# A 7x7 depthwise convolution as one matrix product per tile of pixels, with v laid out in ten dense planes

## The chip, the cores and the metric

The kernel runs on one core of one Trainium2 chip. The metric is the time of one execution on the device in microseconds, lower being better; for a comparison several executions are made and their median is taken. A core has a matrix engine (TensorE, in the profile PE, with its weight loads as PEld), a vector engine (VectorE, DVE), an engine for activations and copies (ScalarE, ACT), a general engine (GpSimd, POOL) and an engine that here issues most of the DMA transfers (SyncE, SP). Each engine executes its own instructions in order and waits on semaphores for what the others produce. SBUF is the memory on the core, PSUM the memory into which matrix products go, HBM the large memory[...].

## The reference

The input `x` has 4 images of 256 channels and 64 x 64 pixels, in float32. Two layers follow each other, each with a group normalization in front and a residual sum behind. The first layer (A below) is an attention of 8 heads of 32 channels over keys and values that come from two 2x2 convolutions of stride 2. The second layer (B) is an attention within each quarter of an image (an area of 16 rows), plus a depthwise 7x7 convolution of its values, and a projection. The part that the change touches is in the second layer:

```python
def _L1_conv_ref(x, w_qkv, b_qkv, w_pe, b_pe, w_proj, b_proj):
    ...
    def _dwconv7(x, w, b):
        y = lax.conv_general_dilated(x, w, window_strides=(1, 1), padding=[(3, 3), (3, 3)], dimension_numbers=('NCHW', 'OIHW', 'NCHW'), feature_group_count=x.shape[1])
        return y + b[None, :, None, None]
    ...
    out = jnp.einsum('bhij,bjhd->bihd', attn, v)
    out = out.reshape(B, N, C)
    v_full = v.reshape(B, N, C)
    out = out.reshape(B, H, W, C).transpose(0, 3, 1, 2)
    v_full = v_full.reshape(B, H, W, C).transpose(0, 3, 1, 2)
    out = out + _dwconv7(v_full, w_pe, b_pe)
    return _conv1x1(out, w_proj, b_proj)
...
x = x + _L0_conv_ref(_gn(x), L0_conv_Wq, L0_conv_Wk, L0_conv_Wv, L0_conv_rel_h, L0_conv_rel_w)
x = x + _L1_conv_ref(_gn(x), L1_conv_w_qkv, L1_conv_b_qkv, L1_conv_w_pe, L1_conv_b_pe, L1_conv_w_proj, L1_conv_b_proj)
```

Each channel has its own 49 taps, and the edges are padded with zeros by 3 pixels.

## The kernel before

**The main loop.** The work is cut into 8 blocks (layer A for the images 0 to 3, then layer B for the images 0 to 3) of 16 units each, 128 units in all. A unit is one chunk of 512 queries (8 rows of an image) and four heads; it has 8 steps, one for each 128 keys. One step issues, in this order: the four score products `s` (`scores`, L261, four row groups side by side), the first of two exponentials on ScalarE (L265), the four products `av` of the step before (`weighted`, L272, four column groups side by side), the second exponential, what the plan holds for this step, and then one or more parts of the side queue. VectorE sums the exponentials of a unit (L797), and after the last step the products with `ones` (`den`, L281) give the divisors. The PSUM tiles of `s` and `den` come from three buffers, all side work shares one PSUM buffer (`side`, L163).

**The plan.** The order is written out by hand. `at(g, j, f)` puts a function into step j of unit g; `task(parts, f)` puts side work of so many parts on the queue `side`, and a function yields where a part ends. In the main loop (L804 to L837) a step takes one part when anything waits, a second when more than 7 parts wait and a third when more than 14 do, one fewer in step 2; further parts in the same step must be of the same task. `need` (L191) takes parts off the queue until something is made. Side parts are the projections of layer A (`k0ps`, `v0ps`, `q0ps`) and B (`k1ps`, `q1ps`), the values of layer B (`vals_ps`), the convolution (`conv_ps`) and the last projection (`ops`). `product` (L151) makes each as four matmuls of 32 output channels side by side.

**The values of layer B.** `plan_values` (L644) loads a chunk of `xmid` (`hv`), normalizes it on ScalarE (L243), makes the products, evicts them with the bias into `vout` (L669, rows of 72 floats: 64 pixels with zeros around them), and, after the second half of the channels, stores the chunk twice: four transfers into `vala` (L677), from which `load_v` and `make_v` (L497, L503) take the values for the attention, and eight, one per row, into `vals` (L682), which holds all rows of all channels and images with the halo, from the last row to the first. The start of each image's chunks in units is given at L771: image 0 from 17.8, image 1 from 48.3, image 2 from 49.8, image 3 from 65.8, with 3.4, 1.0, 1.6 and 0.4 units from chunk to chunk. Before the first of them `plan_zeros` (L616) writes the halo rows of `vals`, zeroes `bands` and puts the taps in with seven transfers.

**The convolution.** `plan_conv` (L695) runs for 64 groups of four channels, from unit 70.5 on, 0.52 units apart. It loads 42 rows of `vals` for each half of the image, three times with a shift of 0, 1 and 2 pixels, into 126 partitions of `rows` (six transfers, L705), and for every second group a tile `band` with the taps as a band matrix (three transfers, L717). For each of two channel pairs and three groups of column shifts it makes four matmuls of 126 rows, 32 output rows and 256 columns (L732: four images of 64 pixels), accumulated over the three column shifts; the task has three parts. One copy (L739) brings 512 columns to SBUF, two transfers (L741) to `conv`. The first load waits with `need(stored, ...)` until the last chunk of values is planned out.

**The rest.** For the images 0 to 2 the attention's result is put aside in `attd` (L548). From unit 105.28 on, 0.8 units apart, `load_rest` (L554) loads a chunk of `conv` (one transfer, L556) and of `attd`, `add_conv` four steps later adds them with the bias (L572), and `project` makes the projection and adds the residual (L583) before `out` is stored (L586). Image 3 does the same behind its own attention.

**DMA.** All these transfers are issued by SyncE in program order. Each takes one of eight semaphores in turn and waits for the transfer that used it last.

## Time and profile before

| | us |
|---|---|
| median of 3 runs | 3268.01 (3267.55 to 3268.94) |
| the profiled execution | 3270.47 |
| its span, from the first to the last instruction | 3268.7 |
| TensorE busy | 3218.2 |
| ScalarE busy | 2525.6 |
| VectorE busy | 2491.6 |
| GpSimd busy | 487.2 |
| exponentials (L265), 2048 of 1027 ns | 2016.9 |
| sums of exponentials (L797), 1792 of 1219 ns | 2113.3 |
| convolution matmuls (L732), 3072 | 195.1 |
| their evictions (L739), 64 of 587 ns | 37.5 |

The granted clock of TensorE was 0.997 over the span. The busy time of a group is the union of its instructions, so concurrent matmuls are counted once; a mean is that of one instruction, and four matmuls that run side by side have each their full length. An f32 matmul of the program stands as two instructions in the trace. In lines of groups the columns are the line, engine and operation, the tiles out<-in with their shapes, the number of instructions, then the busy time and the mean in ns, then the idle time before and what ended it. In timelines they are the start in us, the length, the engine and line, and the tiles.

The DMA page lists 319,853 packets and 397.27 MB, at a mean of 122 GB/s. SyncE's transfers take 38.5% of the sixteen DMA engines' time. A transfer is cut into packets, one for each contiguous run of bytes.

The units of the convolution stage last from about 1787 us (unit 71) to 2663 us (unit 105).

### The profile page before, as it was taken

To read this page: it belongs to the slowest core of one execution; us is meant where nothing else is said; L and a number is where in the kernel's file an instruction comes from. 1 tells how busy PE (TensorE), PEld (TensorE's weight loads), DVE (VectorE), ACT (ScalarE), POOL (GpSimd) and SP (SyncE) were. 2 spreads that over 40 slices of the span, in tenths; PEclk is the share of its full clock that TensorE was granted. 3 is DMA by queue.
4 is the path that set the end of the run, shared out by engine and by line. 5 is a ranking of instruction groups with operands and counts; after the bars stand their busy time and mean duration, and the time that the engine had idled before them with its cause. 6 is when DMAs were issued, how large, how long until landed. Compare 5 with 4: busy or idle time off the path is not lost.

```text
span 3268.7 us, 72561 instructions
## 1 busy us (share of the span) xinstructions
PE 3218.2 (98%) x29730; PEld 961.1 (29%) x29730; DVE 2491.6 (76%) x2621; ACT 2525.6 (77%) x2993; POOL 487.2 (15%) x923
## 2 busy tenths in 40 slices
PE   7999999999999999999999999999999999999997
PEld 4233323333233322222222333333333322222221
DVE  3777897779877787778876767666776778888887
ACT  3888788887888888888887777777777787776765
POOL 0111121111211111111111111111111111111111
PEclk9999999999999999999999999999999999999999
DMA  5312212313322213553236667676766643445431
GB/s 179 80 64 73 77 66 90 100 59 116 100 69 84 65 63 91 148 138 113 82 120 158 162 151 178 159 174 141 180 171 153 172 142 123 166 147 172 155 121 57
DMA packets 319853, 397.27 MB, mean 122 GB/s; under 512 B 182652, under 2 KB 215708, under 8 KB 319192
## 3 DMA queue, kind: packets, MB, share of 16 engines
q1 hardware_dynamic: 291064, 356.06, 38.5%
q0 software_dynamic: 28448, 36.48, 4.2%
q8 instruction: 236, 3.87, 0.5%
q14 instruction: 105, 0.86, 0.1%
HBM read 285.98 MB, written 106.42 MB: 120 GB/s over the span
## 4 chain that ended last, share of the span: by engine, by line
PE 94%; DMA 2%; issue 1%; ACT 1%; DVE 1%; SPq 0%; POOL 0%; DVEq 0%; ACTq 0%; POOLq 0%
PE s L261 33%; PE av L272 29%; PE conv_ps L732 5%; PE den L281 4%; PE k0ps L155 3%; PE k1ps L155 3%; PE q1ps L155 3%; PE v0ps L155 3%; PE q0ps L155 3%; PE ops L155 3%; PE vals_ps L155 3%; ACT p L265 1%; DVE p L797 1%; DMA conv<-cout 0%; DMA rows<-vals 0%
## 5 line engine op out<-in xcount | busy, mean ns | idle before, releaser
L797 DVE TENSOR_TENSOR p<-p 128x1024 f32<-128x1024 f32 x1792 | 2113.3, 1219 | 623.1 <-ACT p L265 583.3
L265 ACT ACTIVATE p<-s 128x1024 f32<-128x1024 f32 x2048 | 2016.9, 1027 | 571.9 <-PE s L261 564.0
L261 PE MATMUL s<-q,k_A 32*128 32x512 f32 x4096 | 608.2, 640 | 1.4 <-ACT p L265 0.9
L261 PE MATMUL s<-q,k_B 32*128 32x512 f32 x4096 | 588.7, 640 | 1.1 <-ACT p L265 0.8
L272 PE MATMUL av<-p,v_A 128*32 128x512 f32 x4096 | 551.1, 603 | 0.0
L272 PE MATMUL av<-p,v_B 128*32 128x512 f32 x4096 | 546.0, 604 | 0.0
L308 POOL DMA_DIRECT2D rb<-recs x508 | 252.4, 502 | 454.1 <-DMA recs<-few 377.5
L306 POOL DMA_DIRECT2D recs<-few x127 | 70.2, 553 | 1423.2 <-DVE sums L305 1372.1
L261 PEld LDWEIGHTS s<-q,k_A 32*128 32x128 f32 x4096 | 176.3, 183 | 357.8 <-issue 273.3
L261 PEld LDWEIGHTS s<-q,k_B 32*128 32x128 f32 x4096 | 162.5, 182 | 363.3 <-issue 290.5
L272 PEld LDWEIGHTS av<-p,v_A 128*32 128x32 f32 x4096 | 89.4, 108 | 383.0 <-issue 335.0
L272 PEld LDWEIGHTS av<-p,v_B 128*32 128x32 f32 x4096 | 87.6, 108 | 378.8 <-issue 332.9
L732 PE MATMUL conv_ps<-rows,band 126*32 126x256 f32 x3072 | 195.1, 379 | 0.0
L732 PEld LDWEIGHTS conv_ps<-rows,band 126*32 126x32 f32 x3072 | 123.0, 139 | 113.0 <-issue 78.3
L297 POOL DMA_DIRECT2D rows<-den_sb x127 | 74.6, 587 | 433.3 <-ACT den_sb L290 424.1
L281 PE MATMUL den<-p,ones 128*32 128x512 f32 x1024 | 137.8, 605 | 0.4 <-DVE p L797 0.4
L155 PE MATMUL ops<-cv,wp_sb 128*32 128x512 f32 x1024 | 129.8, 600 | 6.0 <-issue 6.0
L155 PE MATMUL vals_ps<-hv,wqkv_sb 128*32 128x512 f32 x1024 | 130.1, 596 | 3.9 <-ACT vout L669 3.8
L155 PE MATMUL k0ps<-taps,wk_sb 128*32 128x256 f32 x2048 | 130.6, 383 | 3.0 <-ACT taps L243 3.0
L155 PE MATMUL k1ps<-h,wqkv_sb 128*32 128x512 f32 x1024 | 128.7, 593 | 2.4 <-ACT cout L739 1.6
L155 PE MATMUL q0ps<-hq,wq_sb 128*32 128x512 f32 x1024 | 129.8, 592 | 0.0
L155 PE MATMUL q1ps<-h,wqkv_sb 128*32 128x512 f32 x1024 | 129.7, 596 | 0.1
(87 smaller groups left out, 1594.9 us busy)
## 6 DMA issues: line engine op xcount, KB each, us to landing
rb<-recs POOLq DMA_DIRECT2D x508, 64.0 KB, 2.4
rows<-vals SPq DMA_DIRECT2D x128, 189.0 KB
rows<-vals SPq DMA_DIRECT2D x128, 188.8 KB
rows<-vals SPq DMA_DIRECT2D x128, 188.7 KB
vala<-vout SPq DMA_DIRECT2D x128, 144.0 KB
vals<-vout SPq DMA_DIRECT2D x256, 72.0 KB
vc<-vala SPq DMA_DIRECT2D x32, 576.0 KB
hq<-in_x SPq DMA_DIRECT2D x32, 512.0 KB
```

What stands on the lines that cost most here:

```text
L155: T.matmul(out[cols, :], lhsT=lhsT[:, cols], rhs=rhs, start=start, stop=stop)
L261: T.matmul(pairs[h // 2][:, h % 2, :], lhsT=k[rows, unit[0], j * P : (j + 1) * P], rhs=q[rows, :], start=True, stop=True,)
L265: exps = [lambda i=i: S.activation(p[i], pairs[i], AF.Exp, scale=SCALE) for i in range(2)]
L272: T.matmul(av[HD * h : HD * h + HD, :], lhsT=v[:, j, unit[0] * P + HD * h : unit[0] * P + HD * h + HD], rhs=p[h // 2][:, h % 2, :], start= ...
L281: T.matmul(dens[g][HD * h : HD * h + HD, :], lhsT=ones, rhs=p[h // 2][:, h % 2, :], start=True, stop=True,)
L297: G.dma_start(rows, den_sb[0:P:HD, :])
L306: G.dma_start(recs.rearrange("h (q n) -> (h q) n", n=CH // HD), few[:, 1, :])
L308: G.dma_start(rb[HD * h : HD * h + HD, :], recs[h : h + 1, :].to_broadcast([HD, CH]))
L732: T.matmul(ps[HD * m : HD * m + HD, i], lhsT=band_tiles[k][:, g, :, part + c], rhs=xs[:, m % 2, c, :, 3 * g : 3 * g + WW], start=(g == 0), ...
L797: soon(1, lambda i=i: V.tensor_add(ps[0][i], ps[0][i], ps[j][i]))
```

## The change

The convolution takes tiles of six by four pixels. The rows of `rows` are now the 12 rows and 10 columns around such a tile (120 partitions), the outputs are 24 pixels (padded to 32) for each channel, and the columns of the product run over the tiles: 11 tile rows, 4 images and 16 tiles across. One matmul per channel gives all its outputs of a half (6 or 5 tile rows, 384 or 320 columns), with no accumulation. For this `vals` in HBM holds ten planes, one for each column offset within the window, each dense; a chunk of values is stored into it with ten transfers per half of the channels (`vals` L698 of the changed kernel), given out after each half and not at the end of the chunk. A half's rows are loaded in one transfer (L732), three halves ahead. `bands` has one band of 19 x 13 taps positions for every 16 channels, filled with 49 transfers and loaded with ten. The pixels of `vout`, `vala`, `conv` and `cv` are ordered by their column modulo four, so the copies that make `k`, the transposes that make `v` and the two sums that use `cv` read or write by columns; the eviction of `k` is split in two, and `conv` is loaded with 16 transfers per chunk. The starts of the values and of the convolution are set anew.

```diff
-BAND = HH // 2 + 2 * HALO
-BROWS = 42
-TC = 8
+TY, TX, NY, XT, NP, TC = 6, 4, 11, WW // 4 + 2, 120, 16
+BY, BX = 12 + 7, 10 + 3
...
-    vals = dram.tile([HH + 2 * HALO + BROWS - BAND, C, B, XP], FP, name="vals")
-    vala = [[dram.tile([4, HD, NH, 4, XP], FP, name=f"vala_{b}_{a}") for a in range(NAREA)] for b in range(B)]
-    conv = dram.tile([C, B, N], FP, name="conv")
-    bands = dram.tile([C // TC, 9, BROWS + HH // 2 - 1, TC], FP, name="bands")
+    vals = dram.tile([TY * NY + 2 * HALO, TX + 2 * HALO, C, B, WW // TX], FP, name="vals")
+    vala = [[dram.tile([4, HD, NH, 4 * TX, XT], FP, name=f"vala_{b}_{a}") for a in range(NAREA)] for b in range(B)]
+    conv = dram.tile([C, HD, NY, B, WW // TX], FP, name="conv")
+    bands = dram.tile([C // TC, BY, BX, TC], FP, name="bands")
...
-            S.activation(
-                k[:, qd, :].rearrange("p (j t i) -> p t j i", t=4, i=32)[:, 2 * half : 2 * half + 2],
-                ps.rearrange("p (t j i) -> p t j i", t=2, i=32), AF.Identity, bias=bqkv_sb[:, 1, qd : qd + 1],
-            )
+            for n in range(2):
+                S.activation(
+                    k[:, qd, :].rearrange("p (r g t f x) -> p t r g f x", r=4, g=2, t=4, f=2)[:, 2 * half + n],
+                    ps[:, n * 256 : (n + 1) * 256].rearrange("p (r x g f) -> p r g f x", r=4, g=2, f=2),
+                    AF.Identity, bias=bqkv_sb[:, 1, qd : qd + 1],
+                )
...
-            nc.sync.dma_start(cv, conv[:, b, c * CH : (c + 1) * CH].rearrange("(t p) n -> p t n", p=P))
+            for y in range(c * RC, (c + 1) * RC):
+                n, r = y // TY, TY - 1 - y % TY
+                for t in range(CT):
+                    nc.sync.dma_start(
+                        cv[:, t, :].rearrange("p (f r x) -> p r f x", f=TX, r=RC)[:, y - c * RC],
+                        conv[t * P : (t + 1) * P, r * TX : (r + 1) * TX, n, b, :],
+                    )
...
-                V.scalar_tensor_tensor(cv[:, t, :], cv[:, t, :], bpe_sb[:, t : t + 1], att[:, t, :], ALU.add, ALU.add)
+                V.scalar_tensor_tensor(
+                    by_column(cv[:, t, :]), by_column(cv[:, t, :]), bpe_sb[:, t : t + 1],
+                    att[:, t, :].rearrange("p (q f) -> p q f", f=TX), ALU.add, ALU.add,
+                )
...
-            for n in range(7):
+            for n in range(NTAP):
                 nc.sync.dma_start(
-                    bands[:, :7, BAND - 1 - n, :].rearrange("k x c -> x k c"),
-                    tap[7 * n : 7 * n + 7, :].rearrange("x (k c) -> x k c", c=TC),
+                    bands[:, TY - 1 + n // 7, TX + HALO + 2 - n % 7, :].unsqueeze(0),
+                    tap[n : n + 1, :].rearrange("o (k c) -> o k c", c=TC),
                 )
...
-                vout = made["v"] = pool.tile([P, CT, RC, XP], FP, tag="rows", name=f"vout_{b}_{c}", bufs=2)
+                vout = made["v"] = pool.tile([P, CT, RC, TX, XT], FP, tag="rows", name=f"vout_{b}_{c}", bufs=3)
...
+            for n in range(2):
+                nc.sync.dma_start(
+                    vala[b][c // 2][2 * (c % 2) + n, :, 4 * t : 4 * t + 4].rearrange("c h f x -> h c (f x)"),
+                    vout[:, t, 4 * n : 4 * n + 4].rearrange("p r f x -> p (r f x)"),
+                )
+            for dc in range(TX + 2 * HALO):
+                x, f = divmod(dc + TX - HALO, TX)
+                nc.sync.dma_start(
+                    vals[HALO + c * RC : HALO + (c + 1) * RC, dc, t * P : (t + 1) * P, b, :].rearrange("r p x -> p r x"),
+                    vout[:, t, :, f, x : x + WW // TX],
+                )
             if t == CT - 1:
                 stored[b, c] = True
-                for n in range(2):
-                    for tt in range(CT):
-                        nc.sync.dma_start(
-                            vala[b][c // 2][2 * (c % 2) + n, :, 4 * tt : 4 * tt + 4].rearrange("c h r x -> h c (r x)"),
-                            vout[:, tt, 4 * n : 4 * n + 4, :].rearrange("p r x -> p (r x)"),
-                        )
-                for r in range(RC):
-                    nc.sync.dma_start(
-                        vals[HALO + HH - 1 - c * RC - r, :, b, :].rearrange("(t p) x -> p t x", p=P), vout[:, :, r, :]
-                    )
...
+    halves = ((0, 6), (6, NY))
+    def load_band(k):
+        band = band_tiles[k] = pool.tile([NP, 8, TX * TC], FP, tag="band", name=f"band_{k}", bufs=2)
+        for dc in range(10):
+            nc.sync.dma_start(
+                band[dc::10],
+                bass.AP(
+                    tensor=bands.tensor, offset=bands.offset + (k * BY * BX + 9 - dc) * TC,
+                    ap=[[BX * TC, 12], [BX * TC, 8], [1, TX * TC]],
+                ),
+            )
+    def load_rows(n, half):
+        need(stored, (B - 1, NCH - 1))
+        (lo, hi), row, size = halves[half], C * B * WW // TX, 4 * B * WW // TX
+        loaded[n, half] = xs = pool.tile([NP, 6, 4, B, WW // TX], FP, tag="rows", name=f"rows_{n}_{half}", bufs=3)
+        nc.sync.dma_start(
+            xs.rearrange("p y c b x -> p y (c b x)")[:, : hi - lo],
+            bass.AP(
+                tensor=vals.tensor, offset=vals.offset + TY * lo * 10 * row + n * size,
+                ap=[[row, NP], [TY * 10 * row, hi - lo], [1, size]],
+            ),
+        )
+        if half == 0 and n % (TC // 4) == 1 and n < C // 4 - TC // 4:
+            load_band(n // (TC // 4) + 1)
+    def convolve(n, half):
+        if (n, half) not in loaded:
+            load_rows(n, half)
+        xs, (k, part), (lo, hi) = loaded.pop((n, half)), divmod(4 * n, TC), halves[half]
+        size = (hi - lo) * B * WW // TX
+        ps = ps_side(f"conv_ps_{n}_{half}")[:, :size]
+        for m in range(4):
+            T.matmul(
+                ps[HD * m : HD * m + HD].rearrange("p (y b x) -> p y b x", b=B, x=WW // TX),
+                lhsT=band_tiles[k].rearrange("p y (x c) -> p (y x) c", c=TC)[:, :, part + m],
+                rhs=xs[:, : hi - lo, m], start=True, stop=True,
+            )
+        out = pool.tile([P, 6 * B * WW // TX], FP, tag="cout", name=f"cout_{n}_{half}", bufs=2)[:, :size]
+        S.copy(out, ps)
+        nc.sync.dma_start(
+            conv[4 * n : 4 * n + 4].rearrange("c m y b x -> (c m) y (b x)")[:, lo:hi],
+            out.rearrange("p (y x) -> p y x", y=hi - lo),
+        )
+        n, half = divmod(2 * n + half + 3, 2)
+        if n < C // 4:
+            load_rows(n, half)
+        yield
...
-        at(0, when, load)
-        at(0, when + 4, lambda: task(3, convolve))
-    begin, pace = 70.5, 0.52
+        for half in range(2):
+            if n + half < 2:
+                at(0, int(start * NKT) + 2 * half, lambda half=half: load_rows(n, half))
+            if n + half == 0:
+                at(0, int(start * NKT) - NKT, lambda: load_band(0))
+            at(0, int(start * NKT) + 4 + 2 * half, lambda half=half: task(1, convolve, n, half))
+    begin, pace = 71.3, 0.5
...
-            plan_values(b, c, ends[b] + 1.8 + (14.5 if b == 1 else 0) + (3.4, 1.0, 1.6, 0.4)[b] * c)
+            plan_values(b, c, (17.8, 41, 54.5, 65.8)[b] + (3.0, 1.6, 1.25, 0.5)[b] * c)
```

## What was predicted before the changed kernel ran

> **What bounds the kernel now.** I read the page's first two parts, then the chain of waits, the groups by form, the timeline of TensorE inside the convolution, the stretches by stage, and last the SyncE queue around the stores of v. Parts 1 and 4 first:
>
> ```profile
> PE 3218.2 (98%) x29730; PEld 961.1 (29%) x29730; DVE 2491.6 (76%) x2621; ACT 2525.6 (77%) x2993; POOL 487.2 (15%) x923
> ...
> PE 94%; DMA 2%; issue 1%; ACT 1%; DVE 1%; SPq 0%; POOL 0%; DVEq 0%; ACTq 0%; POOLq 0%
> ```
>
> TensorE is on the chain for 94% of the span. Nothing else is over 77% busy, so time taken out of TensorE is worth its length as long as ScalarE and VectorE keep up and no transfer is late. The stretches by stage (columns: us, PE, PEld, DVE, ACT, POOL, granted clock, DMA share, GB/s) say where:
>
> ```profile
> 1603.00:1787.00 184.00, 182.03 (x1456) 46.47 (x1452) 133.76 (x154) 149.59 (x178) 28.40 (x53) 0.99 0.43 121
> 1787.00:2663.00 876.00, 874.44 (x8772) 294.23 (x8768) 612.94 (x595) 663.50 (x762) 125.79 (x239) 1.00 0.68 163
> 2663.00:3043.00 380.00, 379.92 (x3148) 95.66 (x3144) 318.91 (x343) 278.88 (x310) 54.96 (x105) 1.00 0.45 151
> ```
>
> The middle line is the convolution stage: TensorE full, ScalarE at 76%, DMA at 68%. Its timeline shows the rhythm:
>
> ```profile
> 2209.76 1.14 PE L261 MATMUL s<-q,k_B 32*128 32x512 f32 x8
> 2210.83 1.06 PE L272 MATMUL av<-p,v_B 128*32 128x512 f32 x8
> 2211.72 1.05 PE L732 MATMUL conv_ps<-rows,band 126*32 126x256 f32 x16
> 2212.70 1.14 PE L261 MATMUL s<-q,k_B 32*128 32x512 f32 x8
> ```
>
> A step is one `s`, one `av` and what the side queue adds. With 16 convolution matmuls it lasts 2.94 us (2209.76 to 2212.70). Over all 1023 step starts in the trace, a step with no side part is 2.066 us at least (mean 2.314, ScalarE paces it), with one 512-column part 2.925, with 16 convolution matmuls 2.940, with 32 of them 3.806. So a side part costs only its streaming: four matmuls side by side take 0.429 us per pass of 512 columns (0.859 over two passes), that is 0.839 ns a column, and 0.217 us per pass of 256 columns. An f32 product is two passes.
>
> The last views are the queue of SyncE while image 3's v is stored (its timeline), the chain over one chunk, and the tiles' issue times (ns, least, median, most):
>
> ```profile
> 1690.83 1.68 SPq L677 DMA_DIRECT2D vala<-vout  x3
> 1692.55 5.79 SPq L682 DMA_DIRECT2D vals<-vout  x8
> ```
>
> ```profile
> 1691.99 5.97 DMA vala<-vout
> ...
> 1697.98 2.70 DMA vals<-vout
> ```
>
> ```profile
> L682 SPq DMA_DIRECT2D vals<-vout x256: 359/615/2145, 542.6 to 1786.0; - x128
> L677 SPq DMA_DIRECT2D vala<-vout x128: 503/522/1252, 535.1 to 1778.6; - x128
> L741 SPq DMA_DIRECT2D conv<-cout x128: 574/586/1739, 1809.1 to 2654.9; - x128
> ```
>
> One chunk's stores occupy the queue and the transfers for 8.7 us. The last is issued at 1786.0, the first row load follows it, and the first convolution matmul runs at 1797.9: that hand-over has almost no slack.
>
> [...] matmuls on different column groups of 32 run at once. The trace agrees (four such matmuls start about 7 ns apart), so the convolution is priced by columns, not by matmuls. [...] its packets of 1152 B (53 ns each) go at 80 per us there. [...] The trace has 4-byte packets at 5.9 ns per engine (`tap`, 595 in 0.5 us on 7 engines) and 256-byte packets at 15.7 ns (`conv`, 255 in 0.25 us on 16); no run shows 64 B. [...] The trace's only strided f32 read, `taps` with every second element, took 638 ns for 256 elements where the contiguous groups (819 for 512, 1242 for 1024) give 0.61 us by their slope: no penalty at that stride.
>
> **The change part by part.** Sums are against the profiled execution: 3270.5 us, span 3268.7 and 1.8 around it. The median of the runs shown is 3268.0, 2.5 lower, and I subtract that at the end.
>
> 1. *The matmuls.* Before: 12 passes of 256 columns for each of 64 groups of four channels, in 108 steps of 16 matmuls and 42 of 32. They cost 108 x (2.940 - 2.066) + 42 x (3.806 - 2.066) = 94.4 + 73.1 = 167.5 us. After: two halves of 384 and 320 columns, two passes each, one part per step in 128 steps: 64 x 2 x (384 + 320) x 0.839 ns = 75.6 us. Saved: 91.9 us. The instruction order of the changed program, priced step by step this way, gives 92.1 less. Weight loads stay hidden if 32 columns take the 139 ns shown, since a pass now lasts 0.27 to 0.32 us.
>
> 2. *ScalarE.* Eviction copies: 64 of 587 ns become 64 of 384 and 64 of 320 columns; from 371 ns at 256 columns and 589 at 512 these are 0.479 and 0.425, together +20 us. `k` in two halves: 64 x 689 ns become 128 x about 0.47, +16 us. In the convolution stage that makes about (663.5 + 28) of 784 us, 88%: TensorE still ends last there. The single `side` PSUM buffer now changes hands every step, so each copy must end within the 2 us of the next `s` and `av`; behind two exponentials of 1.03 us it just does. I take +4 us; bounds 0 and 35 (1 us for each of 34 units, as units of little side work show). Four more steps without a side part: +1.
>
> 3. *Values moved in time.* Image 2 began at unit 49.8 and ScalarE waited for its normalization:
>
> ```profile
> L243 ACT ACTIVATE hv<-hv,norm_B 128x512 f32<-128x512 f32 x64 | 52.3, 819 | 7.5 <-POOL norm_B L234 7.5
> ```
>
>    That wait made unit 50 take 6.9 us too long. From 54.5 it is gone; image 3's at 65.8 stays. But units 48 to 64 lose side work, and seven more of them drop to 20.8 us of TensorE, where units have taken 0.9 more because ScalarE paces them: +6.3. Net 0.
>
> 4. *The stores of v.* Per half chunk: 2 `vala` as before and 10 transfers of 1024 packets of 64 B in place of 4 of 256 packets of 288 B; 655,360 small packets instead of 65,536. For images 0, 1 and 2 a chunk has 1.25 units (28 us) or more, which hides them. Image 3 has half a unit. I price a 64-byte packet at 7.1 ns per engine[...], an estimate. On the four engines that also carry `vala` a half then takes 64 x 53 ns + 640 x 7.1 ns = 3.4 + 4.5 = 7.9 us; SyncE needs about as much (10 x 0.6 + 2 x 0.52). The same arithmetic for before gives 8.9 us per chunk, against 8.7 seen. In the changed order (steps priced as in 1, counted from the start of unit 64) the halves are ready from 76 to 177 us and the first convolution stands at 194. From 76: 16 x 7.9 = 126, about 16 for the loads of `hv`, `h`, `vc`, `band` among them, 6 for the first row load: 224. TensorE stands 30 us. ScalarE may show part of it earlier, waiting for `hv`, which queues behind the stores; it is the same time. Bounds: 0 (5.9 ns, with the other loads going beside the stores: 76 + 115 is before 194), and 119 with the 15.7 ns of a 256-byte packet.
>
> 5. *Row loads and bands.* 84,480 packets of 1 KB at about 50 ns replace 16,128 of some 0.3 us: 4.2 against 4.8 ms of engine time, hidden as before, three halves (17 us) ahead.
>
> 6. *The start.* 50 instead of 8 `bands` stores, +15 us of SyncE at 0.36 each, ahead of the loads `xa` and `hq` that unit 4 needs; these have some 15 us of lead: +2, bounds 0 and 8.
>
> 7. *The end stage.* `cv` becomes 16 transfers of 0.43 us to issue: 6.9 us, 9.5 to land, against 12.7 us until VectorE adds it. VectorE has 16% free. +3, bounds 0 and 30 (`ops` and `cv` read by columns at twice 745 ns would bring VectorE level with TensorE). The transpose of `v` and the memsets change form alone.
>
> Sum: 3270.5 - 91.9 + 5 + 0 + 30 + 2 + 3 = 3218.6; less 2.5: **3216 us**.
>
> **Rivals.** *No stall*: 64-byte packets stream at 5.9 ns and the other loads fit beside them on the twelve engines without `vala`. For it: 4-byte packets already go at 5.9 ns; against: 8 transfers in flight at most, and `vala` on four engines. Then 3216 - 30 = 3186. *Stores decide* (the slower side): place, the start of the convolution; price per 64-byte packet x, stall = 16 x (3.4 + 0.64 x) - 96. It eats the whole gain of 82 us (92 - 10) from x = 12 ns. For it: the 256-byte packet's 15.7 ns[...]; against: 32-byte stores took 8 ns in the trace, though never many at once. At 15.7 ns: 3268 - 82 + 119 = 3305. *Strided evictions*: ScalarE and VectorE reading PSUM and SBUF by columns pay double; ScalarE in the convolution stage rises by about 1 us per unit and both stages pace on it: 3216 + 31 + 20 = 3267, no change. That the change does not do what it says is out: the order has 4 x 128 matmuls of 384 and 320 columns in place of 1536 of 256.
>
> **How the numbers follow.** Chances: partial stall 0.52 (3195 to 3250), no stall 0.24, stores decide 0.19, strided evictions 0.05. 0.2% (6.5 us) is about what a measurement of this kernel tells from no change. Faster: 0.52 + 0.24 + 0.01 = 0.77; same: 0.04; slower: 0.19. The range must take in the stall-free case below (3182) and most of the way towards the break-even above (3270); beyond it lie perhaps 0.17 of the slower case and a few hundredths below.
>
> **What would show it.** Steps with a convolution of 2.71 and 2.60 us; ScalarE near 88% in that stage; one wait of TensorE for `rows` at the first convolution, of about 30 us, and `vals` on SyncE at 0.6 us each. If `vals` transfers take over 1 us apiece, or ScalarE waits for `hv` through units 67 to 71, the stores decide and I am too low. If steps of the stage stay near 2.9 us, the exposed copies are the cause.

## The result and the profile after

The changed kernel takes 3413.89 us (median of 4 runs, 3400.47 to 3421.40), the kernel before 3267.78 beside it: a ratio of 1.0442, 95% interval 1.0408 to 1.0477. It is 4.4% slower where 3216 us was forecast. The profiled execution took 3410.18 us with a span of 3408.5.

Parts 1 and 4 of the page after, the engine's busy time and the chain of waits:

```profile
PE 3184.7 (93%) x27682; PEld 887.5 (26%) x27682; DVE 2512.6 (74%) x2621; ACT 2542.3 (75%) x3121; POOL 492.0 (14%) x923
...
PE 71%; SPq 11%; DMA 8%; issue 4%; ACT 3%; DVE 3%; POOL 0%; DVEq 0%; ACTq 0%; POOLq 0%
```

TensorE is busy for less time, as intended, but it is on the chain for 71% of the span and no longer 94%. SyncE's queue and transfers, 2% together before, hold it for 19%. ScalarE's share on the chain is 3%.

Where the rows of the convolution were there in time, its matmuls came out as priced. This is TensorE's timeline in the convolution (start, length, both us):

```profile
2239.73 0.88 PE L749 MATMUL conv_ps<-rows,band 120*32 120x384 f32 x8
2240.55 1.24 PE L263 MATMUL s<-q,k_B 32*128 32x512 f32 x8
2241.72 1.06 PE L274 MATMUL av<-p,v_B 128*32 128x512 f32 x8
2242.60 0.72 PE L749 MATMUL conv_ps<-rows,band 120*32 120x320 f32 x8
2243.26 1.14 PE L263 MATMUL s<-q,k_B 32*128 32x512 f32 x8
...
2248.24 1.07 PE L274 MATMUL av<-p,v_B 128*32 128x512 f32 x8
2251.97 1.30 PE L749 MATMUL conv_ps<-rows,band 120*32 120x320 f32 x8 [2.66 <-DMA rows<-vals]
```

From the `s` at 2240.55 to the next at 2243.26 are 2.71 us, the forecast length of a step with 384 columns; over all steps the medians are 2.71 and 2.61. The last line shows the other side: the next half stands at 2251.97, since its rows were late.

The stretches by stage, from unit 64, the start of unit 71 and the end of the convolution (columns as before):

```profile
1652.20:1865.50 213.30, 187.25 (x1475) 47.18 (x1471) 128.42 (x148) 151.81 (x188) 28.42 (x52) 0.94 0.65 117
1865.50:2768.80 903.30, 812.94 (x6752) 215.90 (x6748) 612.49 (x601) 679.13 (x861) 126.09 (x239) 0.95 0.75 177
2768.80:3171.60 402.80, 385.35 (x3156) 95.88 (x3152) 338.72 (x348) 279.89 (x323) 55.42 (x105) 0.98 0.65 143
```

TensorE was busy for 98.9% or more of each stage before; now it stands for 26, 90 and 17 us (the first convolution falls into the second line). The granted clock, the seventh number, was 0.99, 1.00 and 1.00 in the prediction's lines and is 0.94, 0.95 and 0.98 here.

To see where time is lost I took each step of TensorE from the trace (first `s` to the next first `s`) and subtracted what its matmuls cost by the prediction's prices. The costs sum to 3099.6 us before and 3007.5 after: the 92 us are there. What is left over, the excess, by unit (a unit is one pass over the 8 key tiles):

```
units            4-5    5-64   64-67   67-73   73-76  76-105 105-128     all
before           0.2    37.0     6.3     2.2     0.0     1.9     2.1    53.2
after           22.9    66.3     3.6    96.6     5.7    49.1    35.3   282.9
```

(The 3.5 us of units 0 to 4 are the same in both and only in the sum.) 230 us more than before are lost, in five places: unit 4, the stretch in which images 0 to 2 are stored (units 17 to 63), the hand-over from image 3's stores to the convolution (units 67 to 73), the convolution stage and the end stage. Each column or row of such figures comes from one profiled execution, which can lie up to 10 us from the median of its kernel, so a difference of a few us between two runs tells nothing by itself.

TensorE did not stand for all of these 230 us. Its span less its busy time rose from 50.5 us to 223.8, by 173; the other 57 or so lie in matmuls that took longer. This is where TensorE resumes at the first convolution:

```profile
1945.63 1.52 PE L749 MATMUL conv_ps<-rows,band 120*32 120x384 f32 x8 [37.54 <-DMA rows<-vals]
1947.08 2.09 PE L263 MATMUL s<-q,k_B 32*128 32x512 f32 x8
1949.10 1.94 PE L274 MATMUL av<-p,v_B 128*32 128x512 f32 x8
```

The same three took 0.88, 1.14 and 1.06 us in the timeline above. The granted clock was 0.50 from 1910 to 1951 us, while TensorE stood and for the first 6 us of its work. From 83 us on, the trace has 22 stretches at a granted clock of 0.50, 200 us together, and ahead of each TensorE had stood for 1.4 us or more of the last 4. That alone doesn't tell when the clock falls: at seven other places it had stood as long and the clock stayed at 1.00. The kernel before has 4 stretches at 0.50, with 24 us. TensorE was at work for 92 us of the 200, so at half speed these would cost some 46 us by estimate, most of the 57. So these stalls cost the wait and, by that estimate, slower work behind it. The prediction has no term for that, and no run changes the clock by itself.

*Unit 4.* The chain of the stretch from 165 to 200 us, its shares and four of its 85 pieces (start, length, both us):

```profile
by line: SPq L652 60.1%; DMA xa<-in_x 13.1%; issue 7.7%; PE s L263 5.9%; PE av L274 5.3%; PE v0ps L157 4.8%; ACT p L267 2.9%; SPq L103 1.8%; ACT taps L245 0.1%
...
186.29 0.59 SPq L652
186.92 0.59 SPq L652
187.55 0.59 SPq L103
...
188.26 4.59 DMA xa<-in_x
```

L652 is the store of one tap: 49 of them at 0.63 us apart (31 us), and the load `xa` (L103) stands behind them in the queue.

*The hand-over.* SyncE's timeline over two half chunks and more of image 3:

```profile
1798.45 7.82 SPq L698 DMA_DIRECT2D vals<-vout  x8
1806.38 1.10 SPq L692 DMA_DIRECT2D vala<-vout  x2
1807.53 11.41 SPq L698 DMA_DIRECT2D vals<-vout  x10
1819.36 0.33 SPq L668 DMA_DIRECT2D hv<-xmid  x1
1819.81 1.08 SPq L692 DMA_DIRECT2D vala<-vout  x2
```

and the issue times of `vals` over the whole run (ns, least, median, most):

```profile
L698 SPq DMA_DIRECT2D vals<-vout x640: 363/636/3972, 559.3 to 1938.4; - x160
```

The ten stores of the second half chunk shown took 11.4 us, not 6. The median store is the forecast 0.6 us; the time is in a few long ones, up to 3.97. The chain before the first convolution (1865 to 1952 us) ends with them:

```profile
by line: SPq L698 45.2%; SPq L719 8.9%; PE s L263 8.5%; DMA rows<-vals 7.2%; issue 6.1%; DMA h<-xmid 5.5%; PE av L274 5.4%; SPq L692 4.3%; PE q1ps L157 2.7%; ACT p L267 2.4%; PE conv_ps L749 1.7%; PE vals_ps L157 1.0%; ACT q L531 0.8%; SPq 
...
1929.81 1.65 SPq L698
1931.51 2.73 SPq L698
...
1938.39 0.79 SPq L698
1939.23 6.27 DMA rows<-vals
1945.63 1.52 PE conv_ps L749 x6
```

From 1733 us on the queue gives out stores and the loads among them almost without a break until 1939, then the first rows, and TensorE resumes at 1945.6. Earlier ScalarE had already waited for `hv` behind the same stores (27.6 us in 3 waits between 1600 and 1980; over the whole run 48.1 us, none before).

*The convolution stage.* A piece of the chain there:

```profile
2241.91 0.32 SPq L756
...
2242.34 9.49 DMA rows<-vals
2251.83 0.14 issue
2251.97 1.30 PE conv_ps L749 x7
```

One load of rows took 9.5 us where three steps of 2.7 us, 8.1 us, are the lead. In the kernel before no convolution matmul waited:

```profile
L732 PE MATMUL conv_ps<-rows,band 126*32 126x256 f32 x3072 | 195.1, 379 | 0.0
```

*The end stage.* From the waits of 2760 to 3400 us (total, times, longest) and from the groups by form, after and before (busy us, mean ns):

```profile
PE q1ps L157 <- DVE xm L601: 23.6, 6, 11.0
DVE cv L586 <- DMA at<-attd: 17.2, 4, 7.9
```

```profile
L586 DVE SCALAR_TENSOR_TENSOR cv<-cv,bpe_sb,at 128x512 f32<-128x512 f32 x48 | 52.4, 1138 | 17.2 <-DMA at<-attd 17.2
L572 DVE SCALAR_TENSOR_TENSOR cv<-cv,bpe_sb,at 128x512 f32<-128x512 f32 x48 | 33.8, 745 | 0.0
```

`at` lands late, VectorE then sums late and by columns, and `q` of the next chunk waits for the single side buffer that the projection holds until VectorE has read it.

### The profile page after: what moved, and what is told of

The parts are those of the page before. It is cut to its first block, busy times and chain, and to the rows that moved or that the text cites. A ratio compares the mean times of both kernels' runs of the same rounds, so it can differ in the third digit from the quotient of the medians.

```text
span 3408.5 us, 69491 instructions
## 1 busy us (share of the span) xinstructions
PE 3184.7 (93%) x27682; PEld 887.5 (26%) x27682; DVE 2512.6 (74%) x2621; ACT 2542.3 (75%) x3121; POOL 492.0 (14%) x923
## 4 chain that ended last, share of the span: by engine, by line
PE 71%; SPq 11%; DMA 8%; issue 4%; ACT 3%; DVE 3%; POOL 0%; DVEq 0%; ACTq 0%; POOLq 0%
PE s L263 25%; PE av L274 22%; SPq L698 5%; DMA rows<-vals 4%; SPq L563 3%; PE den L283 3%; PE k0ps L157 3%; PE q1ps L157 3%; PE v0ps L157 3%; PE q0ps L157 3%; PE vals_ps L157 3%; PE k1ps L157 3%; PE ops L157 2%; ACT p L267 2%; DVE p L819 1%
## 5 line engine op out<-in xcount | busy, mean ns | idle before, releaser
L263 PE MATMUL s<-q,k_A 32*128 32x512 f32 x4096 | 616.0, 641 | 35.1 <-ACT p L267 35.1
L263 PE MATMUL s<-q,k_B 32*128 32x512 f32 x4096 | 598.9, 649 | 11.6 <-ACT p L267 11.6
L274 PE MATMUL av<-p,v_A 128*32 128x512 f32 x4096 | 558.2, 607 | 0.0
L157 PE MATMUL q1ps<-h,wqkv_sb 128*32 128x512 f32 x1024 | 138.2, 622 | 42.8 <-DVE xm L601 23.6
L749 PE MATMUL conv_ps<-rows,band 120*32 120x384 f32 (+1 forms) x1024 | 102.1, 469 | 60.2 <-DMA rows<-vals 59.0
L300 POOL DMA_DIRECT2D few<-rows x127 | 72.6, 571 | 447.3 <-DMA rows<-den_sb 442.0
```

The costliest lines, as they stand in the source:

```text
L157: T.matmul(out[cols, :], lhsT=lhsT[:, cols], rhs=rhs, start=start, stop=stop)
L263: T.matmul(pairs[h // 2][:, h % 2, :], lhsT=k[rows, unit[0], j * P : (j + 1) * P], rhs=q[rows, :], start=True, stop=True,)
L274: T.matmul(av[HD * h : HD * h + HD, :], lhsT=v[:, j, unit[0] * P + HD * h : unit[0] * P + HD * h + HD], rhs=p[h // 2][:, h % 2, :], start= ...
L300: G.dma_start(few[:, 0, :], rows.rearrange("h (q n) -> (h q) n", n=CH // HD))
L749: T.matmul(ps[HD * m : HD * m + HD].rearrange("p (y b x) -> p y b x", b=B, x=WW // TX), lhsT=band_tiles[k].rearrange("p y (x c) -> p (y x) ...
```

## The experiments

All times are medians; a ratio is to the kernel before, measured beside it, with its 95% interval. The excess of every run stands in one table at the end of this section. Edits are to the changed kernel unless said otherwise; "..." stands for lines left out.

### The start

```diff
         def taps():
...
-            for n in range(NTAP):
-                nc.sync.dma_start(
+        def store(n):
+            nc.sync.dma_start(
...
+        for n in range(NTAP):
+            at(g + 6, n, lambda n=n: store(n))
```

> The 49 stores of taps are issued one per step from unit 8 on, not all at unit 2. If SyncE's queue held the loads of unit 4 behind them (49 x 0.63 = 31 us), the stall of 22.7 us at unit 4 goes: about 3388 us, with nothing else changed. If the start is late for another reason (the transfers of the first units themselves, or ScalarE), unit 4 keeps its stall and the time stays within 5 us of 3412.

3384.87 us, 1.0350 (1.0332 to 1.0367). The excess of unit 4 fell from 22.9 to 0.2, no other place changed by more than 3.3. The chain around the place (171 to 194 us) is TensorE alone:

```profile
by line: PE s L263 38.1%; PE av L274 32.1%; PE v0ps L157 22.5%; PE den L283 4.3%; PE q0ps L157 3.7%
```

So the tap stores were the whole of the loss in unit 4. The time fell by more than that, 29 us; the four runs of the changed kernel alone lie 21 us apart.

### The stores of v: how many, how large, when

Half the packets in as many issues, the same packets in twice the issues, and image 3's chunks at half the rate with a later convolution:

```diff
e_half
+        for c in range(NCH):
+            for r in range(4):
+                at(16 + 4 * c + r, 3, lambda r=HALO + c * RC + 4 + r: nc.sync.dma_start(vals[r], vals[0]))
...
-                    vals[HALO + c * RC : HALO + (c + 1) * RC, dc, t * P : (t + 1) * P, b, :].rearrange("r p x -> p r x"),
-                    vout[:, t, :, f, x : x + WW // TX],
+                    vals[HALO + c * RC : HALO + c * RC + 4, dc, t * P : (t + 1) * P, b, :].rearrange("r p x -> p r x"),
+                    vout[:, t, :4, f, x : x + WW // TX],
e_dup
-                nc.sync.dma_start(
-                    vals[HALO + c * RC : HALO + (c + 1) * RC, dc, t * P : (t + 1) * P, b, :].rearrange("r p x -> p r x"),
-                    vout[:, t, :, f, x : x + WW // TX],
-                )
+                for n in range(0, RC, 4):
+                    lo = HALO + c * RC + n
+                    nc.sync.dma_start(
+                        vals[lo : lo + 4, dc, t * P : (t + 1) * P, b, :].rearrange("r p x -> p r x"),
+                        vout[:, t, n : n + 4, f, x : x + WW // TX],
+                    )
e_late
-    begin, pace = 71.3, 0.5
-    late, spread = begin + pace * (C // 4) + 1.5, 0.8
+    begin, pace = 75.3, 0.5
+    late, spread = begin + pace * (C // 4) + 1.5, 0.65
-            plan_values(b, c, (17.8, 41, 54.5, 65.8)[b] + (3.0, 1.6, 1.25, 0.5)[b] * c)
+            plan_values(b, c, (17.8, 41, 54.5, 65.8)[b] + (3.0, 1.6, 1.25, 1.0)[b] * c)
```

> Each of the 10 stores of v per half chunk carries only four of its eight rows (512 packets in place of 1024, as many issues); the other four rows of each chunk are left out of the stores and filled with zeros by 32 large copies in units 16 to 47, so the result of the convolution is left incomplete. If the packets are short, image 3's stall of 96 us goes almost wholly, and the small stalls in images 1 and 2 with it: 3290 to 3320 us. If the issues are short, image 3 keeps at least 80 us of stall: 3390 us or more.

> Each store of v is given out as two of 512 packets in place of one of 1024: the same packets, 20 issues per half chunk in place of 10. If SyncE's time per issue is what is short (0.64 us each), image 3's stores need another 16 x 10 x 0.6 = 96 us and the stall about doubles: 3500 us or more. If the packets are what is short (10 to 11 ns each on 16 engines, 0.65 us per 1024), an issue takes half as long and the time stays at 3400 to 3425 us.

> Image 3's chunks of v come one per unit in place of one per half unit, the convolution begins 4 units later, and the end stage is drawn together (0.65 units per chunk). Theory Q (image 3's stores need some 15 us per chunk and a half unit gives 12): the 96 us of stall in units 68 to 71 go almost wholly, about 3320 us, and no wait for rows stays at the first convolution. Rival E (the 64-byte stores disturb whatever runs beside them, wherever they are): the stall is spread over units 66 to 75 and less than 40 us is won, over 3370 us. The conv stage's own 55 us should stay in both.

`e_half`: 3330.49 us, 1.0181 (1.0164 to 1.0198). `e_dup`: 3541.03 us, 1.0835 (1.0817 to 1.0853). `e_half` met neither theory: with half the packets the stall falls from 96.6 to 55.2, which is neither almost gone nor 80 and more. `e_dup` met the total that the theory of short issues gave, 3500 or more, but not by its reason: the stall grows by 48 where 96 was expected, and 82 more are lost in the stretch of images 0 to 2 (66.3 to 148.6; with half the packets 31.1). Issue times of `vals` in the two (ns, least, median, most):

```profile
L701 SPq DMA_DIRECT2D vals<-vout x640: 359/517/3067, 560.2 to 1863.9; - x160
```

```profile
L700 SPq DMA_DIRECT2D vals<-vout x1280: 359/513/3432, 560.8 to 2076.5; - x183
```

An undisturbed issue costs 0.51 us with 512 packets and 0.61 with 1024, so most of it does not go with the packets, and twice the issues cost dear. The mean store fell from 1.02 us to 0.77 with half the packets: 0.10 of that is the undisturbed issue, the rest long issues that became shorter or fewer.

`e_late`: 3401.86 us, 1.0393 (1.0372 to 1.0415). In total that is rival E's number (over 3370, less than 40 us won), but by its places it isn't E: the excess of units 67 to 76 falls from 102.3 to 40.9, most of the way that theory Q said, as a backlog would, while the end stage, drawn together behind the later convolution, pays 79.0 in place of 35.3. The total of an experiment that moves a stage hides what it was meant to show; the places do not.

### Where the long issues come from

In the trace of the changed kernel I put the 12 issues of each half chunk on SyncE in order. Medians in ns, for the second half chunk of a chunk in images 0 to 2 and for image 3:

```
place              vala vala  vals ...
second halves       522  514   619 2408 2793  582  607  606  609  711  631  807
image 3             543  518   548 2138 2687  582  605  607  631  751  611  761
```

In these medians it is the second and third store of `vals`. The two of `vala` ahead differ from the rest in how many packets run at a time. In this trace one or more of `vala`'s stores' packets, of 1152 bytes (the 53 ns of the prediction; 51 in the median here), were under way for 264 us, and for 155 of these it was four: hence "on four engines". Packets of 64 bytes ran 12 or 13 at a time most often (147 of the 942 us with any), those of 2 KB 16 (96 of 380 us), the number of DMA engines by which the page counts. Three edits ask whether `vala` is the cause: `vala` last, `vala` with the head ahead of the channel, `vala` from another queue. That the second form runs on 16 engines, as it is called here, is an estimate from the transfers of 2 KB packets, which lie over 128 partitions as its stores do.

```diff
e_last
-            for n in range(2):
-                nc.sync.dma_start(
-                    vala[b][c // 2][2 * (c % 2) + n, :, 4 * t : 4 * t + 4].rearrange("c h f x -> h c (f x)"),
...
             for dc in range(TX + 2 * HALO):
...
+            for n in range(2):
+                nc.sync.dma_start(
+                    vala[b][c // 2][2 * (c % 2) + n, :, 4 * t : 4 * t + 4].rearrange("c h f x -> h c (f x)"),
...
e_vala16
-    vala = [[dram.tile([4, HD, NH, 4 * TX, XT], FP, name=f"vala_{b}_{a}") for a in range(NAREA)] for b in range(B)]
+    vala = [[dram.tile([4, NH, HD, 4 * TX, XT], FP, name=f"vala_{b}_{a}") for a in range(NAREA)] for b in range(B)]
...
-                    vala[b][c // 2][2 * (c % 2) + n, :, 4 * t : 4 * t + 4].rearrange("c h f x -> h c (f x)"),
+                    vala[b][c // 2][2 * (c % 2) + n, 4 * t : 4 * t + 4].rearrange("h c f x -> (h c) (f x)"),
...
-            nc.sync.dma_start(
-                vcs[a, half], vala[b][a][:, :, half * NH // 2 : (half + 1) * NH // 2].rearrange("t c h f x -> (t c) h f x")
-            )
+            for n in range(4):
+                nc.sync.dma_start(
+                    vcs[a, half][HD * n : HD * n + HD],
+                    vala[b][a][n, half * NH // 2 : (half + 1) * NH // 2].rearrange("h c f x -> c h f x"),
+                )
e_valapool
             for n in range(2):
-                nc.sync.dma_start(
+                G.dma_start(
                     vala[b][c // 2][2 * (c % 2) + n, :, 4 * t : 4 * t + 4].rearrange("c h f x -> h c (f x)"),
```

> The two stores of vala of a half chunk are issued after its ten stores of vals, not before. In the changed kernel the second and third vals store of each half chunk hold SyncE for 2.0 and 2.7 us, the others for 0.6. Theory R (the packets of vala, 53 ns each on four engines[...]): the long issues go from these places, a half chunk takes about 8 us of SyncE in place of 11.3, image 3's stall falls by 16 x 3 = 48 us and images 1 and 2 lose most of their 34 us: about 3330 to 3350 us. Rival P (any ten stores of 1024 packets of 64 bytes take 10 to 11 us, whatever goes before them): the long issues move to other places, the time stays within 15 us of 3412.

> vala is kept with the head ahead of the channel[...] (its loads become four transfers each in place of one). Theory R ([...] four engines work off vala's packets, and the second and third vals store wait for it): the long issues of 2.0 and 2.7 us fall to 0.6 to 0.9, a half chunk takes 8 to 8.5 us of SyncE in place of 11.3, image 3's stall of 96 us falls by about 48 and the 34 us of images 1 and 2 by 20 or more: 3335 to 3355 us. Rival P (1024 packets of 64 bytes cost 0.65 us of 16 engines each and vala adds the same bytes wherever it runs): the long issues stay or move, less than 15 us are won: over 3395 us.

> The stores of vala are issued from the queue of GpSimd, as they were otherwise; the stores of vals stay with SyncE. Theory R1[...]: vals issues are 0.6 us throughout, about 3340 us, as with vala on 16 engines. Rival R2 (the four engines themselves are late, whichever queue feeds them): the second and third vals store still take about 2 us, 3390 us or more. GpSimd's own small transfers for the divisors may come later in both.

`e_last`: 3435.14 us, 1.0510 (1.0492 to 1.0527). As a repair it failed and the expected 3330 to 3350 missed, but its trace is clear. SyncE's timeline of the first chunk of all, in the changed kernel, with `vala` last, and with `vala` on 16 engines:

```profile
558.02 1.21 SPq L692 DMA_DIRECT2D vala<-vout  x2
559.29 9.12 SPq L698 DMA_DIRECT2D vals<-vout  x10
571.28 1.10 SPq L692 DMA_DIRECT2D vala<-vout  x2
572.42 14.30 SPq L698 DMA_DIRECT2D vals<-vout  x10
```

```profile
559.75 6.66 SPq L693 DMA_DIRECT2D vals<-vout  x10
566.45 1.19 SPq L698 DMA_DIRECT2D vala<-vout  x2
570.32 13.38 SPq L693 DMA_DIRECT2D vals<-vout  x10
```

```profile
558.93 0.80 SPq L694 DMA_DIRECT2D vala<-vout  x2
559.77 6.75 SPq L700 DMA_DIRECT2D vals<-vout  x10
568.40 0.97 SPq L694 DMA_DIRECT2D vala<-vout  x2
569.42 12.27 SPq L700 DMA_DIRECT2D vals<-vout  x10
```

With no `vala` ahead, ten stores take 6.66 us; in the second half, which now follows the first half's `vala`, they take 13.38. In the medians of images 0 to 2 the first halves have no issue over 0.70 us, the second halves 2.10 and 3.16 at the second and third. Moving `vala` moved the wait to where nothing was gained. Not all of it is `vala`'s: with `vala` on 16 engines the second half of this chunk still takes 12.27 us.

`e_vala16`: 3349.40 us, 1.0247 (1.0230 to 1.0264), as theory R said (3335 to 3355). The long issues of image 3 fall from 2.14 and 2.69 us to 0.75 and 1.50, a half chunk from 11.3 to 9.0 us of issues, the stall from 96.6 to 63.6, and the excess of units 5 to 64 from 66.3 to 31.6. It is below the 37.0 of the kernel before, so all that the change had added in the stretch of images 0 to 2 is gone. A part of the long issues stays in second halves (2.1 us at one place in the median); no run shows why.

`e_valapool`: 3419.63 us, 1.0444 (1.0415 to 1.0473): R2. Without `vala` in SyncE's queue the third `vals` store of second halves still takes 3.1 us in the median, and ten stores take 10.5 to 11.6 us of issues. In theory R1 it was `vala`'s place in SyncE's queue that counted. As far as this run tells, `vala`'s stores need not stand in SyncE's queue to hold it up; how an issue comes to wait for them is not shown.

One more edit took image 3's `vals` off SyncE:

```diff
             for dc in range(TX + 2 * HALO):
                 x, f = divmod(dc + TX - HALO, TX)
-                nc.sync.dma_start(
+                (G if b == B - 1 else nc.sync).dma_start(
```

> Image 3's stores of vals are issued from GpSimd's queue, not SyncE's; all else is as in the changed kernel. Theory Q (loads of hv, h, vc and band stand behind the stores in SyncE's queue): SyncE has 10 us less per half chunk, the 33 us of units 67 to 70 go, and the stall at the first convolution is set by the transfers alone, 9.8 us per half chunk on the four engines with vala: 76 + 157 + 6 - 194 = 45 us; about 3360 us. Rival P (the packets' own time sets it): the sum of the stall in units 67 to 73 stays above 80 us, 3395 us or more. If GpSimd is slower than 0.65 us at giving out 1024 packets, it is over 3410 us.

3447.12 us, 1.0549 (1.0532 to 1.0567), the last of the three outcomes: in this run GpSimd took 0.88 us to issue each of these stores, and the stall grew to 126.8. It says nothing on theory Q.

### The convolution and end stages

```diff
e_rows
...
-        loaded[n, half] = xs = pool.tile([NP, 6, 4, B, WW // TX], FP, tag="rows", name=f"rows_{n}_{half}", bufs=3)
+        loaded[n, half] = xs = pool.tile([NP, 6, 4, B, WW // TX], FP, tag="rows", name=f"rows_{n}_{half}", bufs=4)
-        if half == 0 and n % (TC // 4) == 1 and n < C // 4 - TC // 4:
+        if half == 0 and n % (TC // 4) == 2 and n < C // 4 - TC // 4:
...
-        n, half = divmod(2 * n + half + 3, 2)
+        n, half = divmod(2 * n + half + 4, 2)
...
-                at(g - 3, 2 + 5 * half, lambda a=a, half=half: load_v(a, half))
-                at(g - 2, 2 + 4 * half, lambda a=a, half=half: make_v(a, half))
+                at(g - 3, 2 + 11 * half, lambda a=a, half=half: load_v(a, half))
+                at(g - 2, 2 + 7 * half, lambda a=a, half=half: make_v(a, half))
...
e_end
+            att = None
+            if b < B - 1:
+                att = chunk_tile(f"at_{b}_{c}")
+                nc.sync.dma_start(att, attd[b][c])
             cv = chunk_tile(f"cv_{b}_{c}")
...
-            if b < B - 1:
-                att = chunk_tile(f"at_{b}_{c}")
-                nc.sync.dma_start(att, attd[b][c])
...
-                at(g, j + 4, lambda c=c: add_conv(c))
-                at(g, j + 6, lambda c=c: soon_tasks([(2, project, c, to) for to in range(CT)]))
+                at(g, j + 6, lambda c=c: add_conv(c))
+                at(g, j + 8, lambda c=c: soon_tasks([(2, project, c, to) for to in range(CT)]))
e_flat
-            return a.rearrange("p (f q) -> p q f", f=TX)
+            return a
...
-                    att[:, t, :].rearrange("p (q f) -> p q f", f=TX), ALU.add, ALU.add,
+                    att[:, t, :], ALU.add, ALU.add,
...
-            x_to = xm[:, to, :].rearrange("p (q f) -> p q f", f=TX)
+            x_to = xm[:, to, :]
```

> Row loads are issued four halves ahead of their convolution, in four buffers in place of three (the tile that v is read back into keeps one buffer in place of two, and its second half is loaded and transposed some steps later, to make room). Theory L (in the stretches where convolutions stand in successive steps of 2.7 us a row load of 8 to 9.5 us is later than three steps): the 45 us of excess in units 76 to 105 fall to about 15: 3375 to 3385 us. Rival B (the single side buffer and cout's two buffers hold the matmuls): 5 us or less are won, 3405 us or more.

> In the end stage the load of at is issued ahead of the 16 transfers of cv, and the sum over cv and its projection come two steps later. Theory L (VectorE starts late since at and cv land late behind 16 issues of 0.5 us): the 32 us of excess in units 112 to 128 fall by 15 or more: 3395 us or less. Rival V (VectorE's sums by columns, 1.14 us in place of 0.74, make it late by themselves): less than 6 us, 3405 us or more.

> The two sums of the end stage read cv and the product of the projection in order and no longer by columns: the permutation of the pixels is left out, so the output's pixels stand in the wrong places. Theory V (strided reading on VectorE): both sums fall from 1.14 us to 0.74 and the end stage's 32 us of excess fall by 15 or more: 3395 us or less. Rival L (late loads): less than 6 us, 3405 us or more.

`e_rows`: 3400.32 us, 1.0400 (1.0382 to 1.0417). The total lies between the two theories. Units 76 to 105 fall from 49.1 to 26.1, about three quarters of what theory L said; units 64 to 67 give 8 back, where `vc` has one buffer. The depth of the loads was about half of the excess here. Of the rest, ScalarE's copies wait for `cout`'s two buffers for 30.4 us between 1600 and 2700 in the changed kernel; a run below returns to it.

`e_end`: 3434.14 us, 1.0501 (1.0484 to 1.0519): worse, which no theory said. SyncE's own waits in its end stage (total, times, longest) say why:

```profile
SPq L567 <- DVE cv L586: 41.5, 5, 16.2
```

L567 is the load of `cv`. It stood for 41.5 us until VectorE had freed a chunk tile, and with it the whole queue. A later sum holds its tiles longer, and six were just enough.

`e_flat`: 3400.10 us, 1.0408 (1.0387 to 1.0428). Units 105 to 128 fall from 35.3 to 24.4: the columns are worth 11 us here, a third. Only one of the two sums had been slow: the one over `cv` went from 1138 to 746 ns, while the one over `ops`, which reads PSUM by columns, had taken 750 in the changed kernel (749 before). The waits for `at` stayed (17.3 us).

### Together

The repairs are put on top of each other: `e_pair` has the edits of `e_taps`, `e_vala16` and `e_rows`. `e_cvrows` adds the first edit below, `e_b1` the second, `e_b2` both.

```diff
e_cvrows
-            cv = chunk_tile(f"cv_{b}_{c}")
+            cv = pool.tile([P, CT, CH], FP, tag="rows", name=f"cv_{b}_{c}", bufs=4)
-                at(g, j + 4, lambda c=c: add_conv(c))
-                at(g, j + 6, lambda c=c: soon_tasks([(2, project, c, to) for to in range(CT)]))
+                at(g, j + 8, lambda c=c: add_conv(c))
+                at(g, j + 10, lambda c=c: soon_tasks([(2, project, c, to) for to in range(CT)]))
e_b1
-    begin, pace = 71.3, 0.5
+    begin, pace = 73.3, 0.5
-            plan_values(b, c, (17.8, 41, 54.5, 65.8)[b] + (3.0, 1.6, 1.25, 0.5)[b] * c)
+            plan_values(b, c, (17.8, 41, 54.5, 65.8)[b] + (3.0, 1.6, 1.25, 0.7)[b] * c)
```

> The taps' stores one per step, vala on 16 engines, and row loads four halves ahead in four buffers, together. If the stalls are separate, as their places say, the gains add: 22.7 at unit 4, 18 in units 76 to 105, and what vala on 16 engines gives alone (about 68 by theory R, under 15 by rival P): 3412 - 41 - 68 = about 3303 us, or 3360 to 3371 us by the rival.

> Taps one per step, vala on 16 engines and rows four ahead as before; in addition the tiles of cv lie in the four buffers that the rows of the convolution leave free, so that cv and at can be loaded eight steps ahead of the sum in place of four. Theory L (the end stage's stalls at units 115, 119 and 123 come from at and cv landing late, and the earlier trial to wait longer only ran out of chunk tiles): the 36 us of excess in units 112 to 128 fall by 15 or more, 3293 us or less against 3308. Rival V (VectorE's sums by columns and its transposes of v collide there however early the loads are): less than 6 us, over 3300 us.

> Taps one per step, vala on 16 engines, rows four ahead, and the convolution begins 2 units later (73.3) with image 3's chunks every 0.7 unit. Theory Q (what is left of the stall, 63 us in units 67 to 73, is backlog of the 16 half chunks at 9.4 us, 150 us of SyncE in some 118 us): it falls to 25 us or less, and the end stage is 2 units later at the same pace, costing 5 to 15: 3275 to 3290 us. Rival E (the stores delay the loads beside them wherever they stand): less than 15 us are won, over 3293 us.

> The two edits of the runs beside it together: the later begin and the longer lead of the end stage's loads. If both stalls are what theories Q and L say, 3255 to 3275 us, level with the kernel before; if the later begin pushes the end stage's side work past the last unit, the gain of the begin is given back and it is over 3290 us.

`e_pair`: 3307.70 us, 1.0123 (1.0105 to 1.0140), against 3303 from adding the separate gains. `e_cvrows`: 3281.40 us, 1.0033 (1.0022 to 1.0045); the end stage falls from 39.4 to 7.6, so late loads for want of tiles were its main part. `e_b1`: 3295.04 us, 1.0065 (1.0049 to 1.0082); the stall of units 67 to 73 falls from 63.4 to 14.1, which is theory Q, and the end stage gives 28 of it back, where 5 to 15 were expected; so the total is 5 us above theory Q's range. `e_b2`: 3257.70 us, 0.9964 (0.9949 to 0.9979), a little faster than the kernel before: of the 92 us that the matmuls save, 12 arrive. From its waits between 1600 and 2700 us, TensorE's only one for rows, and ScalarE's for the buffers of `cout`:

```profile
ACT cout L762 <- DMA conv<-cout: 33.9, 23, 3.2
...
PE conv_ps L756 <- DMA rows<-vals: 8.1, 1, 8.1
```

In the changed kernel TensorE's waits for rows in those 1100 us were 15, 56.5 us in all, 37.5 in the longest. The other line asks for two more runs: a third buffer for `cout` on top of `e_b2`, and with it a begin between the two.

```diff
e_cout
...
-        out = pool.tile([P, 6 * B * WW // TX], FP, tag="cout", name=f"cout_{n}_{half}", bufs=2)[:, :size]
+        out = pool.tile([P, 6 * B * WW // TX], FP, tag="cout", name=f"cout_{n}_{half}", bufs=3)[:, :size]
e_b4
-    begin, pace = 73.3, 0.5
+    begin, pace = 72.6, 0.5
-            plan_values(b, c, (17.8, 41, 54.5, 65.8)[b] + (3.0, 1.6, 1.25, 0.7)[b] * c)
+            plan_values(b, c, (17.8, 41, 54.5, 65.8)[b] + (3.0, 1.6, 1.25, 0.6)[b] * c)
```

> As e_b2, with three buffers for cout in place of two. Theory C (what is left in the convolution stage is ScalarE's copy waiting for the store two halves earlier, 33.9 us in 23 waits): the 31 us of excess in units 76 to 105 fall by 12 or more, 3235 to 3247 us against 3258. Rival S (the queue itself is short there, so the row loads take the place of the stores as what is late): less than 5 us are won, over 3252 us.

> As e_cout, with the convolution begun at 72.6 in place of 73.3 and image 3's chunks every 0.6 unit. If the 26 us of the end stage come from starting it late, and the hand-over keeps a backlog of 16 half chunks at 9.4 us, the end stage gains about 9 (0.7 of a unit's side work) and the hand-over loses about 15 (0.7 unit): within 10 us of e_cout. If it is more than 10 us faster, the hand-over still had room at 73.3.

`e_cout`: 3228.14 us, 0.9880 (0.9865 to 0.9895): the excess of units 76 to 105 goes from 30.9 to 3.7, twice what theory C asked for. Part 4 of its page, the chain of waits:

```profile
PE 85%; SPq 4%; DVE 3%; issue 3%; DMA 3%; ACT 1%; POOL 0%; DVEq 0%; ACTq 0%; POOLq 0%
```

`e_b4`: 3274.00 us, 1.0016 (1.0009 to 1.0023), 46 us above `e_cout` and outside both expectations: the hand-over loses the 16 that were priced, but the convolution and end stages lose 16 and 13 as well. So the end stage's rest isn't the price of a late begin; what it is, and why these two stages are so sensitive to the begin, stays open. The waits of `cout` for its stores are back in `e_b4` (20.7 us in 7), with three buffers, so a third buffer does not end these waits at every begin.

The excess of all runs, us by units:

```
units            4-5    5-64   64-67   67-73   73-76  76-105 105-128     all
after           22.9    66.3     3.6    96.6     5.7    49.1    35.3   282.9
e_taps           0.2    68.5     3.6    99.9     5.6    52.2    35.0   268.4
e_late          23.4    66.1     3.6    23.9    17.0    57.8    79.0   274.2
e_dup           23.5   148.6     9.1   145.1     3.8    43.3    34.5   411.4
e_half          24.6    31.1     3.6    55.2     4.8    51.8    35.6   210.3
e_last          24.0    86.2     3.6   103.4     3.4    50.3    33.0   307.3
e_rows          23.0    64.8    11.5    97.3     2.5    26.1    35.9   264.8
e_end           24.4    74.1     3.6    99.6     3.3    51.4    49.4   309.4
e_flat          23.2    66.2     5.3    97.4     3.2    51.1    24.4   274.2
e_vala16        23.5    31.6     5.3    63.6     3.4    54.0    35.7   220.5
e_valapool      22.8    85.5     3.6    86.7     5.2    52.3    35.5   295.1
e_pool          24.5    66.7     3.6   126.8     3.7    52.1    34.5   315.5
e_pair           0.2    31.4     9.4    63.4     1.8    33.8    39.4   182.8
e_cvrows         0.2    33.6     8.3    64.4     2.3    38.0     7.6   157.9
e_b1             0.2    32.8     9.0    14.1     9.9    42.4    67.5   179.5
e_b2             0.2    33.3    10.3    12.8    10.6    30.9    25.6   127.2
e_cout           0.2    32.1     7.7    12.7     9.2     3.7    28.9    97.8
e_b4             0.2    36.4     8.6    29.2     6.0    19.9    42.4   146.3
```

## Why the prediction was wrong

The direction was wrong. The first step of the prediction was right, and four of its terms that lie on transfers were far too small. Of its own signs, the steps of 2.71 and 2.61 us came true, and so did both for being too low: a store of `vals` took 1.02 us in the mean to issue, and ScalarE waited for `hv` in units 67 to 71.

1. *The matmuls*, −91.9: right. The steps' costs fell by 92.1, and weight loads stayed hidden (142 ns each).
2. *ScalarE*, +5: the copies took 0.490 and 0.437 us for 0.479 and 0.425 priced, and `k`'s halves 474 ns for 0.47. Its busy time in the stage, 679 us, is near the forecast 691, and it is 3% of the chain. The rival of strided evictions fell with it, as far as ScalarE goes.
3. *Values moved*, 0: image 2's wait went, units 64 to 67 got 2.7 better; near enough. No run tests it alone.
4. *The stores of v*, +30: this is the step that failed. The failing term is the 7.9 us for a half chunk; a half chunk took 11.8 from first to last issue (median of image 3). Put into the step's own sum it gives 76 + 16 x 11.8 + 16 + 6 - 194 = 93, and 94.4 more than before were lost (TensorE stood for about 80 of them, the rest were slower matmuls). That the packet was mis-sized is not shown. The 7.1 ns priced for a packet of 64 bytes were the author's estimate; of them the trace before shows the 5.9 alone, as the pace of 4-byte packets of `tap`, which start every 5.9 ns in groups of seven there. In the trace after, packets of 64 bytes are recorded with 10 ns in the mean, but those of `tap` are recorded with 9.6 before; the densest half microsecond after has 1082 packets of 64 bytes, 7.4 ns each on 16 engines. Even 10 ns gives only 61 by the rival's formula. The rest is what the prediction treated as two sums side by side, the engines' time and SyncE's: the second and third store after `vala` took 3.6 us more than the rest (2.14 and 2.69 us for 0.61 each), about what `vala`'s two stores take on four engines by the step's own sum, 3.4. `e_vala16` shows this share: −33 at the hand-over. `e_b1`, with a later begin on top, shows the backlog: 63.4 became 14.1. The step's "images 0 to 2 hide them" failed for the same reason: 29 us were lost there, and `e_vala16` removed all of it. The likely way: their chunks have 28 us or more, but the two half chunks of one now hold the queue for 22 to 29 us, with at most 3.3 between them, and a load that falls behind them is late; ScalarE waited 20 us for `hv` before 1600 us, none in the kernel before.
5. *Row loads hidden*: wrong, 47 us in units 76 to 105. The time of the engines was counted, not the time of one load: a row load took 9.5 us in the piece shown, where three steps take 8.1. Its packets are recorded with 73 ns in the mean where 50, an estimate that no trace shows, was priced; the 1 KB packets of `band` before had 82. The average pace (a half every 6 us) would have hidden it; the convolutions come in runs of successive steps. `e_rows` won 23 of it, and `e_cout`, with the begin of `e_b2`, most of the rest: with two buffers ScalarE's copies waited for the stores of `cout` (33.9 us in 23 waits in `e_b2`), which the prediction didn't count at all.
6. *The start*, +2: 22.7. The 49 stores were priced at 0.36 us, the time of the seven wider ones before; a store of one tap took 0.59, 0.63 with the gap. At 31 us the 15 us of lead are gone. `e_taps` gave back all.
7. *The end stage*, +3: 33. The upper bound, 30, was near; the value taken was the other end. `e_flat` gives 11 of it to reading by columns: 1.14 us a sum of `cv` where it was 745 ns. The elements of `taps`, where the prediction found no effect (638 ns against 0.61 us), lay 8 bytes apart, those of `cv` lie 512 apart; no run shows at which distance it begins or why. `e_cvrows` won 32 of it (39.4 to 7.6) with the columns as they are, by loads that have tiles enough to start early; there, the columns can cost no more than the 5.5 us that are left over the 2.1 of before. With the later begin (`e_b2`, `e_cout`) more is lost in this stage again, 26 and 29, and the cause is open.

The sum with measured terms: 22.7 + 29.3 - 2.7 + 94.4 + 5.7 + 47.2 + 33.1 = 229.7, less 92.1 is +138; the span grew by 139.8. The rival of the slower side named the largest of the places but put it down to the price of a packet (12 ns and more); at the recorded 10 ns it would not have decided. Four sums under-priced in the same direction did. The slower matmuls behind these stalls (2.09 us for 1.14 at the first convolution), which had no term at all, are inside the measured terms.

## What to carry to other kernels

When a change multiplies small transfers, price the queue in order, not the totals: write down which load stands behind which burst, how long the burst holds the queue and how early the load is issued. Look for the transfer that holds up the ones behind it and change its form first: here `vala`'s stores, four packets at a time, stood ahead of issues of 2.14 and 2.69 us, and the other layout made these 0.75 and 1.50 and the whole 64 us shorter (3413.89 to 3349.40). Size loads and buffers for the rate of successive steps, not the mean rate. With all this mended (`e_cout`) the same change is 1.2% faster than the kernel before: 41 of the 92 us that the matmuls save arrive. With a begin 0.7 units earlier (`e_b4`) it is only level, so that gain is not robust.

## What the runs showed of the hardware that was not expected

- An issue on SyncE took about 0.51 us with 512 packets of 64 bytes and 0.61 with 1024, so most of it does not go with the packets; a store of one partition with 16 packets took 0.59.
- The second and third store issued after `vala`'s two, whose packets ran four at a time for 155 of 264 us, took 2.1 to 2.8 us to issue in the medians of second halves and of image 3, up to 4; with `vala`'s other layout (`e_vala16`) 0.75 and 1.5 in image 3, and up to 2.1 in second halves. With `vala` issued from GpSimd's queue (`e_valapool`) the third still took 3.1 us in second halves.
- In `e_pool` GpSimd took 0.88 us to issue a store of 1024 packets of 64 bytes.
- Packets of 64 bytes (918,288, nearly all of them the stores of `vals` and the loads of `cv`) were recorded with 10 ns in the mean. In the densest half microsecond they were recorded with 11 ns, which makes 24 of them at a time, where the page counts 16 engines; the 4-byte packets of `tap` were recorded with 9.6 ns where they started every 5.9 ns in groups of seven. So such records were longer than the pace. The row loads' packets of 1 KB were recorded with 73 ns, those of `band` in the kernel before with 82.
- VectorE's sum of 512 f32 elements took 1.14 us when it read one operand in SBUF and wrote its result at steps of 512 bytes, and 745 ns in order. Reading PSUM by columns showed no cost here: VectorE's sum over `ops` took 750 ns, 749 before, and ScalarE's eviction of 512 elements 699 ns, 696 before.
- In 22 stretches of 3 to 41 us, each behind 1.4 us or more of standing within 4 us, TensorE's granted clock was 0.50; behind as much standing at seven other places it stayed at 1.00. A group of matmuls that took 1.14 us at 1.00 took 2.09 behind the longest stall.
